# Four row sums moved from TensorE to accumulating DMAs, with the preparation reordered, in a four-layer graph kernel

## The chip, the cores and the metric

The kernel runs on one core of a Trainium2 chip. The metric is device time of one launch, in microseconds; lower is better. The core has five instruction streams that run side by side and meet only at semaphores: TensorE (PE in the profile, with its weight loads as PEld), VectorE (DVE), ScalarE (ACT), GpSimd (POOL) and SyncE (SP). Each stream runs its instructions in the order in which they were written; an instruction that waits holds up everything behind it on its own engine. DMAs are issued by one of these streams and then run on their own.

## The reference

The input is `x`, 32 samples of 512 nodes with 256 features in float32, and one adjacency matrix `adj` (512 x 512, integers). Four layers follow each other; each adds its result to `x` after a layer norm with a ReLU:

```python
h = jnp.maximum(_layernorm(x, axis=-1), 0.0)
x = x + _L3_gnn_ref(h, adj, adj[None], L3_gnn_W, ...)      # layers 0, 1, 2 likewise
```

Layer 0 is masked attention with four heads. Layer 1 is an MLP with two graph attentions. Layer 2 is a graph attention with four heads of 64 features, layer 3 one with eight heads of 32 features and a prior made of `adj`. For each head of layers 2 and 3 the score of a pair of nodes is a sum of two numbers, one of the row and one of the column, under a leaky ReLU:

```python
e = jax.nn.leaky_relu(e_src[..., :, None] + e_dst[..., None, :], ALPHA)
attn = jax.nn.softmax(e, axis=-1)
h = jnp.einsum('bhij,bhjf->bhif', attn, x_proj)
```

## The kernel before

First comes a preparation: it loads the weights, turns `adj` into four masks (`mask1`, `mask0T`, `mask1T`, `mask3T`), multiplies attention vectors into the weights, and computes a flag `go` that says whether the fast path may be taken. Then all engines branch, and `pipelined` runs. (`general`, the other branch, does not run on these inputs.)

In `pipelined` the four layers of each sample are recorded as steps by a planner, `Plan`. The planner puts the steps of all samples into one order by a list schedule of its own: it has a cost for each step (`cost`), release times for samples and layers (`STARTS`, `PACE`, `LAYERS`), due times (`PERIOD`, and the shifts in `URGENT`) and a stock of buffers (`BLOCKS` tiles of 128 x 512 float32, four `x` tiles, eight banks of PSUM). Steps of up to four samples stand interleaved on every engine. `_Recorder.__getattr__` (line 261) records each step and so is the line that the profile shows for all of them; the tiles tell them apart.

Layers 2 and 3 go through `separable`. After the layer norm, `node_major` computes values and scores of 128 nodes at a time; ScalarE copies the scores to the tile `e`. Four transposes bring the row scores to one row a head (`pt<-ident,e`), ScalarE copies them to `rT`, a DMA writes them to DRAM (`rd`), and one DMA a head broadcasts a row to 128 partitions (`R<-rd`). Heads are worked off in groups `g` of four. For each of the four blocks `j` of 128 keys and each head `s`, ScalarE makes `p = exp(R + e)`, VectorE takes the maximum with the other branch of the leaky ReLU and applies the mask (`p<-p,e,mask3T`), and TensorE multiplies with the values: four matmuls of 32 columns each, one a head, run beside each other in the array as one unit ("columns").

The denominators of the softmax are sums over the keys. In group 0, VectorE adds the four `p` of a head into `total`, and TensorE sums `total` over partitions in one unit with a matrix of ones. In group 1, which only layer 3 has, nothing is added beforehand: TensorE runs a unit of four sum matmuls for every `j`, accumulating in the PSUM bank `sm`:

```python
if not added:
    for s in range(4):
        q.tensor.matmul(sm[s * F3 : (s + 1) * F3, :], ones[:, :F3], p[s], **st)
```

`normalise` then copies `sm`, sends it through DRAM for a reciprocal and a broadcast, and multiplies (`oT<-raw,rc`).

In layer 1, `first_gat` needs two numbers a node. TensorE leaves four partial rows each in `part`; four matmuls with the selection matrix `pick` sum them into `f1p`, and VectorE copies the eight columns to `sd`.

GpSimd has only two kinds of steps in the pipeline: the power that ends each layer norm's statistics (`rs<-ve,mhalf`, four a sample) and the addition of a bias to `x` in layer 0 (`x<-x,boa`). VectorE's next step of that norm, `ms`, waits for `rs`, then ScalarE's `h`, then TensorE's transposes `pt<-ident,h`.

A first load of `x` can be issued by SyncE only when the preparation's buffers are free, since the `x` tiles lie in the pool `big`, which is opened where the pool `prep` was.

Of the kernel before, what the change touches and what calls it, by code (L numbers as in the profile page):

```python
# [11 lines left out]
F32 = mybir.dt.float32  # L12
# [18 lines left out]
G = 2  # L31
# [10 lines left out]
PERIOD = 51.0  # L42
STARTS, PACE = (0.0, 8.0, 36.0, 32.0), 110.0
LAYERS = (0.0, 51.0, 151.0, 201.0)

URGENT = {
    "stats:0": 76, "h:0": 358, "mm:0": 3, "sc:0": 60, "p0:0": -99, "av:0": 39, "stats:1": -269, "pt:1": 119,
    "nd:1": -201, "total:1": 12, "av:1": -22, "e:1": -39, "o2:1": 73, "s:1": -189, "pt:2": 15, "e4:2": -44,
    "total:2": 10, "stats:3": -38, "mv:3": -56, "mm:3": -12, "p3:3": -178, "total:3": -169, "sm:3": 86,
    "s1:3": -16,  # L50
}
BLOCKS, KEEP = 60, 2
# [244 lines left out]
def cost(engine, op, args, kw, out):  # L297
# [22 lines left out]
    if engine == "POOL":  # L320
        return (1.0 if n < 16 else 0.683), 0.1
# [7 lines left out]
def gnn_stack_kernel(ctx: ExitStack, tc: tile.TileContext, a: dict, out: bass.AP):  # L329
# [29 lines left out]
    def load_col(name, eng):  # L359

        src = a[name]
        t = const.tile([P, src.shape[0] // P], F32, name=name)
        eng.dma_start(t, T(src, "(k p) -> p k", p=P))
        return t

# [19 lines left out]
    bq8 = const.tile([P, KD], F32, name="bq8")  # L385

# [6 lines left out]
    pick = const.tile([P, 2], F32, name="pick")  # L393
# [9 lines left out]

    prep_stack = ExitStack()
    prep = prep_stack.enter_context(tc.tile_pool(name="prep", bufs=2))
    pp = prep_stack.enter_context(tc.tile_pool(name="prep_psum", bufs=1, space=PSUM))
    with prep_stack, tc.manual_schedule():

        adj = prep.tile([P, NT, N], I32, name="adj", bufs=1)
        nc.gpsimd.dma_start(adj, T(a["adj"], "(t p) j -> p t j", p=P))  # L410
# [3 lines left out]
        nc.sync.dma_start(a2, bass.AP(tensor=src.tensor, offset=src.offset, ap=[[0, P], [1, 2 * F2]]))  # L414
        s3 = load_bcast(prep, "L3_a_src", nc.sync, D)
        d3 = load_bcast(prep, "L3_a_dst", nc.sync, D)
        wq = load_rows("wqT", nc.scalar, D)
        rows = []
        for name in ("bq", "bk"):
            t = prep.tile([1, D], F32, name=f"{name}r")  # L420
            nc.sync.dma_start(t, a[name][None, :])
            rows.append(t)
        for k in range(KD):
            nc.scalar.dma_start(
                T(w3[:, k, H3 : H3 + D], "p (h f) -> p h f", h=H3), T(a["L3_W"][:, k * P : (k + 1) * P, :], "h p f -> p h f")
            )
        wk = load_rows("wkT", nc.scalar, D)
        bt = load_bcast(prep, "beta", nc.sync, 1)
        bq = load_col("bq", nc.sync)
        bk = load_col("bk", nc.sync)  # L430
        afc = load_bcast(prep, "a_fc", nc.sync, 2 * HID)
        wo = load_rows("woT", nc.scalar, D)
        wv = load_rows("wvT", nc.scalar, D)
        wfc = load_rows("W_fc", nc.scalar, HID)
        bo = load_bcast(const, "bo", nc.sync, D)
        bv = load_bcast(const, "bv", nc.sync, D)
        bvc = prep.tile([P, KD], F32, name="bvc")
        nc.sync.dma_start(bvc, T(a["bv"], "(k p) -> p k", p=P))
        ahd = load_bcast(prep, "a_hand", nc.sync, 2 * D)
        b1 = load_col("mlp1_b", nc.sync)  # L440
        b2 = load_col("mlp2_b", nc.sync)
        wh = load_rows("W_hand", nc.scalar, D + 2)
        m1 = load_rows("mlp1_w", nc.scalar, HID)
        m2 = load_rows("mlp2_w", nc.scalar, D)
        w3o = load_rows("L3_WoT", nc.scalar, D)
# [10 lines left out]
        for c in range(2):  # L456
            nc.vector.tensor_reduce(pick[:, c : c + 1], ident[:, c:P:32], axis=AX.X, op=ALU.add)


        top = prep.tile([P, NT], F32, name="top")  # L460
        adjf = prep.tile([P, NT, N], F32, name="adjf", bufs=1)
        for t in range(NT):
            nc.vector.tensor_copy(adjf[:, t, :], adj[:, t, :])
        adjT = []
        for j in range(NT):
            pt = pp.tile([P, N], F32, name="adjT", bufs=NT)
            for t in range(NT):
                nc.tensor.transpose(pt[:, t * P : (t + 1) * P], adjf[:, t, j * P : (j + 1) * P], ident)
            adjT.append(pt)
        for t in range(NT):  # L470
            nc.vector.tensor_reduce(top[:, t : t + 1], adjf[:, t, :], axis=AX.X, op=ALU.max)
            nc.vector.tensor_scalar(mask1[:, t, :], adjf[:, t, :], 0.0, -BIG, op0=ALU.is_le, op1=ALU.mult)


        ab = prep.tile([P, 1], F32, name="ab")
        nc.vector.tensor_scalar(ab, bt, -1.0, None, op0=ALU.mult)
        nc.vector.tensor_tensor(ab, ab, bt, op=ALU.max)
        nc.scalar.activation(ab, ab, AF.Exp, scale=-1.0)
        m3 = [prep.tile([P, N], F32, name="m3", bufs=NT) for _ in range(NT)]
        for j in range(NT):  # L480
            nc.scalar.activation(m3[j], adjT[j], AF.Relu)
        nc.scalar.activation(ab, ab, AF.Ln, bias=one)

        ok = prep.tile([P, NT], F32, name="ok")
        nc.vector.tensor_scalar(ok, top, 0.0, None, op0=ALU.is_gt)
        nc.vector.tensor_scalar(top, top, 0.0, None, op0=ALU.max)
        nc.scalar.activation(top, top, AF.Ln, bias=eps)
        for j in range(NT):
            nc.scalar.activation(m3[j], m3[j], AF.Ln, bias=eps)
        nc.vector.scalar_tensor_tensor(beta, bt, 0.0, ab, op0=ALU.max, op1=ALU.add)  # L490

        for j in range(NT):
            nc.scalar.activation(m3[j], m3[j], AF.Exp, scale=beta)
# [9 lines left out]
        for w, h, f, vs, vd in (  # L503
            (w2, H2, F2, a2[:, 0:1, :].to_broadcast([P, H2, F2]), a2[:, 1:2, :].to_broadcast([P, H2, F2])),
            (w3, H3, F3, T(s3, "p (h f) -> p h f", h=H3), T(d3, "p (h f) -> p h f", h=H3)),
        ):
            project(lambda k: w[:, k, h : h + D], KD, h, f, vs, lambda k: w[:, k, :h])
            project(lambda k: w[:, k, h : h + D], KD, h, f, vd, lambda k: w[:, k, 3 * h + D :])
            nc.vector.tensor_scalar(w[:, :, h + D : 2 * h + D], w[:, :, :h], ALPHA - 1.0, None, op0=ALU.mult)
            nc.vector.tensor_scalar(w[:, :, 2 * h + D : 3 * h + D], w[:, :, 3 * h + D :], ALPHA, None, op0=ALU.mult)  # L510


# [3 lines left out]
        for w, row in zip((wq, wk), rows):  # L516
            gp = pp.tile([64, N], F32, name="gp", bufs=2)
            for h in range(4):
                c = slice(h * 64, (h + 1) * 64)
                for k in range(KD):  # L520
                    nc.tensor.matmul(gp[:, c], w[:, k, c], w[:, k, c], start=(k == 0), stop=False)
                nc.tensor.matmul(gp[:, c], row[:, c], row[:, c], start=False, stop=True)
# [4 lines left out]
        for n in range(2):  # L527
# [5 lines left out]
        gab = prep.tile([64, D], F32, name="gab")  # L533
        nc.vector.tensor_copy(gab, gp[:, :D])
        nc.vector.tensor_tensor(gab, gab, gp[:, D:], op=ALU.mult)
        nc.vector.tensor_reduce(
            tests[:64, 2 * H + 1 : 2 * H + 5], T(gab, "p (h f) -> p h f", h=4), axis=AX.X, op=ALU.add
        )
# [6 lines left out]
        nc.vector.tensor_tensor(tests[:, : 2 * H], sq[:, 0, :], sq[:, 1, :], op=ALU.add)  # L545
        bad = prep.tile([P, NT], F32, name="bad")
# [18 lines left out]
        for j in range(NT):  # L565
            nc.vector.tensor_scalar(mask0T[:, j, :], adjT[j], 0.0, None, op0=ALU.not_equal)
            nc.vector.tensor_scalar(mask1T[:, j, :], adjT[j], 0.0, None, op0=ALU.is_gt)
        nc.vector.tensor_scalar(bq8, bq, 0.125, None, op0=ALU.mult)
# [5 lines left out]
        nc.vector.tensor_tensor(boa, bo, tp[:, :D], op=ALU.add)  # L574
        for j in range(NT):
# [26 lines left out]
    def pipelined(stack):  # L602
# [158 lines left out]
        def first_gat(o1):  # L761
# [10 lines left out]
            f1p = bank("f1p")  # L772
            for t in range(NT):
                q.tensor.matmul(f1p[:, 2 * t : 2 * t + 2], part[:, col(t)], pick, start=True, stop=True)
            q.vector.tensor_copy(T(sd, "p t c -> p (t c)"), f1p[:, : 2 * NT])
# [113 lines left out]
        def separable(xt, w, nh, mask, bars):  # L889
# [3 lines left out]
            e = small(f"e{nh}", NT, 3 * nh)  # L893
            v = blocks("vs", 2)
            for t in range(NT):
                ps = node_major(w, t, hT, nh, D + 2 * nh)
                q.scalar.copy(half(v, t), ps[:, :D])
                q.scalar.copy(e[:, t, : 2 * nh], ps[:, D : D + 2 * nh])
            q.scalar.activation(e[:, :, 2 * nh :], e[:, :, nh : 2 * nh], AF.Exp, scale=1.0 / ALPHA)
            pt = bank("pt")  # L900
            for t in range(NT):
                q.tensor.transpose(pt[:nh, col(t)], e[:, t, :nh], ident)
            rT = block("rT")
            q.scalar.copy(rT[:nh, :], pt[:nh, :])
            rd = q.tile(dram, [H3, N], "rd", 6)
            q.sync.dma_start(rd[:nh, :], rT[:nh, :])
            per = P // f
            for g in range(nh // 4):
# [4 lines left out]
                added = g == 0  # L913
                if added:
                    total = blocks("total", 4)
                else:
                    sm = bank("sm")
                for j in range(NT):
                    p = blocks("p3", 4)
                    for s in range(4):  # L920
                        h = 4 * g + s
                        q.scalar.activation(p[s], R[s], AF.Exp, bias=e[:, j, nh + h : nh + h + 1])
                        q.vector.scalar_tensor_tensor(
                            p[s], p[s], e[:, j, 2 * nh + h : 2 * nh + h + 1], mask[:, j, :], op0=ALU.max, op1=ALU.mult
# [477 lines left out]
```

## Time and profile before

| what | before |
|---|---|
| time, median of 3 runs | 4181.78 us (4181.32 to 4182.27) |
| time of the profiled execution | 4184.13 us |
| its span, from first to last instruction | 4182.3 us |
| TensorE busy | 4059.5 us, 97% |
| VectorE busy | 3312.1 us, 79% |
| ScalarE busy | 3004.7 us, 72% |
| GpSimd busy | 254.8 us, 6% |
| mean DMA rate | 43 GB/s |
| sum matmuls of group 1 (`sm<-p,ones`) | 1024 instructions, 142.1 us busy |
| sum matmuls of `total` (`sm<-total,ones`) | 768 instructions, 104.0 us busy |
| `R<-rd` | 384 DMAs of 256 KB |

Busy time is what an engine spent on instructions; the engines overlap, so the rows do not add up to the span. A float32 matmul against 512 columns shows as two instructions in the profile. An instruction's mean duration is longer than the distance at which the next one starts, because matmuls are pipelined; the distance between starts is what a matmul costs where TensorE is the limit. Idle time of an engine costs nothing unless the chain that ends last runs through it.

### The profile page before, as it was taken

The page shows a single profiled execution, that of the slowest core. Times are in us where ns is not written, and L with a number is a line of the kernel's source. Part 1 is how long each engine was busy: PE and PEld are TensorE (multiplying, and loading weights), DVE is VectorE, ACT ScalarE, POOL GpSimd, SP SyncE. Part 2 cuts the span into 40 slices and gives each one's busy share as a digit, 9 for nine tenths or more (in the row PEclk, how much of TensorE's full clock was granted, in tenths as well). Part 3 has the DMA queues.
Part 4 walks back from the last instruction along what each step waited for, and adds up shares of the span by engine and source line. Part 5 has one row for each costly group of instructions (what it writes and reads, how often), then busy time and mean ns, then how long its engine had stood idle before and what let it go on. Part 6 is the DMA issues. An engine that isn't in the chain of part 4 may idle for free.

```text
span 4182.3 us, 52787 instructions
## 1 busy us (share of the span) xinstructions
PE 4059.5 (97%) x17862; PEld 2068.7 (49%) x17862; DVE 3312.1 (79%) x7018; ACT 3004.7 (72%) x5970; POOL 254.8 (6%) x263
## 2 busy tenths in 40 slices
PE   5999999999999999999999999999999999999986
PEld 3545454554454554455554455554455554455442
DVE  5388877878877878877879877879877878877876
ACT  3467777766777766777766777776777776787774
POOL 1000000000000000000000000000000000000000
PEclk7999999999999999999999999999999999999998
DMA  2001111111110111110111111111111111111111
GB/s 84 11 21 47 47 47 33 49 52 32 47 51 30 49 52 32 47 52 30 49 52 32 47 52 31 47 52 32 47 52 32 46 52 32 47 52 32 41 42 52
DMA packets 149435, 181.07 MB, mean 43 GB/s; under 512 B 45858, under 2 KB 81572, under 8 KB 149156
## 3 DMA queue, kind: packets, MB, share of 16 engines
q1 hardware_dynamic: 143572, 172.37, 13.5%
q10 hardware_dynamic: 5312, 4.20, 0.3%
q8 instruction: 143, 2.34, 0.2%
q14 instruction: 136, 1.11, 0.1%
q0 software_dynamic: 272, 1.05, 0.1%
HBM read 158.41 MB, written 19.14 MB: 42 GB/s over the span
## 4 chain that ended last, share of the span: by engine, by line
PE 78%; DVE 13%; DMA 4%; ACT 2%; issue 1%; SPq 0%; POOL 0%; DVEq 0%; POOLq 0%
PE mm L261 36%; PE av L261 26%; PE pt L261 6%; PE sc L261 5%; PE sm L261 4%; DVE p L261 3%; DVE total L261 3%; DVE ue L261 2%; DMA rc<-s 2%; DVE o L261 2%; PE f1p L261 1%; DVE oT L261 1%; ACT p L261 1%; DVE x L261 1%; DMA s<-few 1%; DMA R<-rd 1%
## 5 line engine op out<-in xcount | busy, mean ns | idle before, releaser
L261 ACT ACTIVATE p<-R,e 128x512 f32<-128x512 f32 x1536 | 1010.2, 721 | 167.7 <-DMA R<-rd 167.5
L261 DVE SCALAR_TENSOR_TENSOR p<-p,e,mask3T 128x512 f32<-128x512 f32 x1024 | 718.2, 745 | 368.1 <-ACT p L261 367.9
L261 PE MATMUL av<-p,v 128*64 128x512 f32 (+1 forms) x2048 | 689.8, 597 | 1.4 <-DVE p L261 1.4
L261 DVE TENSOR_TENSOR total<-total,p 128x512 f32<-128x512 f32 x832 | 547.2, 680 | 0.0
L261 PE MATMUL av<-p,vs 128*32 128x512 f32 (+1 forms) x3072 | 524.8, 598 | 19.2 <-DVE p L261 19.1
L261 PE MATMUL mm<-W_fc,o 128*128 128x512 f32 x1024 | 467.0, 593 | 0.0
L261 PEld LDWEIGHTS av<-p,v 128*64 128x64 f32 (+1 forms) x2048 | 257.5, 163 | 363.4 <-issue 297.1
L261 POOL TENSOR_TENSOR rs<-ve,mhalf 128x4 f32<-128x4 f32 x128 | 151.0, 1180 | 3764.2 <-DVE ve L261 3593.1
L261 DVE SCALAR_TENSOR_TENSOR p<-p,e,mask1T 128x512 f32<-128x512 f32 x512 | 367.6, 742 | 5.8 <-ACT p L261 5.4
L261 ACT ACTIVATE h<-x,ms,rs 128x256 f32<-128x256 f32 x512 | 269.7, 593 | 128.7 <-DVE ms L261 128.7
L261 DVE TENSOR_TENSOR p<-p,mask0T 128x512 f32<-128x512 f32 x512 | 324.1, 681 | 38.3 <-ACT p L261 38.3
L261 PEld LDWEIGHTS av<-p,vs 128*32 128x32 f32 (+1 forms) x3072 | 135.8, 119 | 346.0 <-issue 239.0
L261 PEld LDWEIGHTS mm<-W_fc,o 128*128 128x128 f32 x1024 | 188.9, 190 | 210.0 <-issue 183.4
L261 DVE TENSOR_TENSOR total<-p,p 128x512 f32<-128x512 f32 x416 | 278.9, 678 | 1.0
L261 ACT ACTIVATE p<-sc 128x512 f32<-128x512 f32 x512 | 262.9, 687 | 7.7 <-PE sc L261 7.7
L261 PE MATMUL mm<-w,hT 128*128 128x272 f32 (+1 forms) x1024 | 262.3, 398 | 1.8 <-ACT hT L261 1.8
L261 PE MATMUL av<-pT,v 128*128 128x512 f32 x512 | 239.9, 593 | 0.5 <-ACT pT L261 0.4
L261 PE MATMUL mm<-o,mlp_w 128*128 128x512 f32 x512 | 228.8, 598 | 0.0
L261 PE MATMUL sc<-qT,kT 64*128 64x512 f32 x1024 | 228.3, 595 | 0.0
L261 PE MATMUL mm<-hT,mlp_w 128*128 128x512 f32 x512 | 225.7, 592 | 0.0
L261 PEld LDWEIGHTS mm<-w,hT 128*128 128x128 f32 x1024 | 188.1, 193 | 54.8 <-ACT hT L261 10.3
L261 ACT COPY sums<-sm 128x512 f32<-128x512 f32 x96 | 55.8, 581 | 195.8 <-PE sm L261 195.7
(187 smaller groups left out, 6076.5 us busy)
## 6 DMA issues: line engine op xcount, KB each, us to landing
R<-rd SPq DMA_DIRECT2D x384, 256.0 KB
x<-in_x_dram SPq DMA_DIRECT2D x32, 512.0 KB
rc<-s SPq DMA_DIRECT2D x128, 128.0 KB
rc<-s SPq DMA_DIRECT2D x256, 64.0 KB
out_dram<-x SPq DMA_DIRECT2D x32, 512.0 KB
s<-sums SPq DMA_DIRECT2D x96, 8.0 KB
few<-s SPq DMA_DIRECT2D x96, 8.0 KB
s<-few SPq DMA_DIRECT2D x96, 8.0 KB
```

Of the source, the lines that this page charges most:

```text
L261: getattr(getattr(self.nc, attribute), op)(*args, **kw)
```

## The change

- In group 1 of layer 3, VectorE's four `p` of block 0 become accumulators (`first`). For blocks 1 to 3, GpSimd issues a DMA that adds `p[s]` to `first[s]` in SBUF: 12 DMAs of 256 KB a sample, 384 in all. TensorE sums the accumulators in one unit at the end, as it does with `total` in group 0. An accumulating DMA waits for the matmul that reads `first[s]` as values' weights, for its own `p[s]`, and for the DMA before it on the same `first[s]`.
- In `separable`, the row scores go to a tile of their own (`es`), so that one transpose does for all four node blocks, with a smaller `rT`; the copies from PSUM become two small ones.
- In `first_gat`, four transposes of `part` and a VectorE reduction take the place of the four matmuls with `pick` and the copy.
- In the preparation, `adj` is loaded by SyncE in four pieces, most weights by SyncE and the two `L3_W` pieces by GpSimd; five bias vectors come as one row and are turned by 12 small matmuls; the transposed `adj` is copied to SBUF by ScalarE, and the masks are made from that copy; the projection of `w2` moves ahead of the masks, and `mask1` behind `go`.
- The `x` tiles get a pool of their own (`first`), opened before `prep`.
- The planner's numbers change (`PERIOD`, `STARTS`, `PACE`, `LAYERS`, `URGENT`, 59 blocks for 60), and with them the order of all steps.

```diff
-PERIOD = 51.0
-STARTS, PACE = (0.0, 8.0, 36.0, 32.0), 110.0
-LAYERS = (0.0, 51.0, 151.0, 201.0)
+PERIOD = 54.0
+STARTS, PACE = (0.0, 6.0, 22.0, 46.0), 81.0
+LAYERS = (0.0, 31.0, 185.0, 164.0)
...
-BLOCKS, KEEP = 60, 2
+BLOCKS, KEEP = 59, 2
...
     if engine == "POOL":
+        if op == "dma_start":
+            return 1.2, 3.0
...
+    first = ctx.enter_context(tc.tile_pool(name="first", bufs=1))
...
-        nc.gpsimd.dma_start(adj, T(a["adj"], "(t p) j -> p t j", p=P))
+        av = T(a["adj"], "(t p) j -> p t j", p=P)
+        for t in range(NT):
+            nc.sync.dma_start(adj[:, t, :], av[:, t, :])
...
+        projections(w2, H2, F2, a2[:, 0:1, :].to_broadcast([P, H2, F2]), a2[:, 1:2, :].to_broadcast([P, H2, F2]))
...
+            at = prep.tile([P, N], F32, name="at", bufs=NT)
+            nc.scalar.copy(at, pt)
+            adjT.append(at)
...
+        projections(w3, H3, F3, T(s3, "p (h f) -> p h f", h=H3), T(d3, "p (h f) -> p h f", h=H3))
...
+        for c in range(12):
+            nc.tensor.matmul(cp[:, c : c + 1], row[:, c * P : (c + 1) * P], ones[:1, 0:1], start=True, stop=True)
+        nc.vector.tensor_copy(biases, cp[:, :12])
...
-            f1p = bank("f1p")
-            for t in range(NT):
-                q.tensor.matmul(f1p[:, 2 * t : 2 * t + 2], part[:, col(t)], pick, start=True, stop=True)
-            q.vector.tensor_copy(T(sd, "p t c -> p (t c)"), f1p[:, : 2 * NT])
+            pt = bank("pt")
+            for t in range(NT):
+                q.tensor.transpose(pt[:, col(t)], part[:, col(t)], ident)
+            q.vector.tensor_reduce(sd, T(pt, "p (t k c) -> p t c k", k=KH, c=32)[:, :, :2, :], axis=AX.X, op=ALU.add)
...
-                q.scalar.copy(e[:, t, : 2 * nh], ps[:, D : D + 2 * nh])
+                q.scalar.copy(es[:, t * nh : (t + 1) * nh], ps[:, D : D + nh])
+                q.scalar.copy(e[:, t, :nh], ps[:, D + nh : D + 2 * nh])
...
-            for t in range(NT):
-                q.tensor.transpose(pt[:nh, col(t)], e[:, t, :nh], ident)
-            rT = block("rT")
-            q.scalar.copy(rT[:nh, :], pt[:nh, :])
+            q.tensor.transpose(pt[: NT * nh, :P], es, ident)
+            rT = q.tile(big, [P, P], "rT", 4, tag="turned")
+            q.scalar.copy(rT[: NT * nh, :], pt[: NT * nh, :P])
...
-                        if added and j:
+                        if j and total:
                             q.vector.tensor_tensor(total[s], first[s] if j == 1 else total[s], p[s], op=ALU.add)
-                    if added and not j:
+                        elif j:
+                            q.gpsimd.dma_start(out=first[s], in_=p[s], accum_op=ALU.add)
+                    if not j:
                         first = p
...
-                        if not added:
-                            for s in range(4):
-                                q.tensor.matmul(sm[s * F3 : (s + 1) * F3, :], ones[:, :F3], p[s], **st)
-                if added:
-                    sm = bank("sm")
-                    with q.unit("columns", 0.86):
-                        for s in range(4):
-                            q.tensor.matmul(sm[s * F3 : (s + 1) * F3, :], ones[:, :F3], total[s], start=True, stop=True)
+                sm = bank("sm")
+                with q.unit("columns", 0.86):
+                    for s, b in enumerate(total or first):
+                        q.tensor.matmul(sm[s * F3 : (s + 1) * F3, :], ones[:, :F3], b, start=True, stop=True)
...
-            xt = q.tile(big, [P, NT, D], "x", 4)
+            xt = q.tile(first, [P, NT, D], "x", 4)
```

## The prediction

> **What bounds the kernel now.** I read the page first, then stretches of the steady state, then the chain of waits inside one sample's period, then the groups by form, and last the start in order of time.
>
> The page: span, TensorE's share, its granted clock by slices, and the chain that ended last.
>
> ```profile
> span 4182.3 us, 52787 instructions
> PEclk7999999999999999999999999999999999999998
> PE 78%; DVE 13%; DMA 4%; ACT 2%; issue 1%; SPq 0%; POOL 0%; DVEq 0%; POOLq 0%
> ```
>
> TensorE carries the chain, and its clock is full but for the first and last slices. The stretches (PE, PEld, DVE, ACT, POOL busy, then clock, DMA share and rate):
>
> ```profile
> 400.00:640.00 240.00, 239.31 (x1072) 121.91 (x1071) 195.87 (x418) 180.86 (x363) 15.48 (x16) 1.00 0.14 43
> 3700.00:3890.00 190.00, 188.66 (x878) 94.37 (x877) 160.86 (x326) 141.39 (x279) 9.20 (x9) 1.00 0.13 40
> 4100.00:4183.00 83.00, 53.69 (x216) 22.26 (x208) 46.13 (x91) 31.77 (x62) 1.34 (x1) 0.84 0.17 53
> ```
>
> From 70 to 3890 us TensorE is never free; VectorE has about a fifth of its time left. So work taken from TensorE is time, until VectorE's order or a wait steps in. The period of a sample, from the timeline of TensorE: the sums that close first_gat's softmax start at 2009.39 and again at 2134.51, so 125.1 us a sample.
>
> ```profile
> 2009.39 0.95 PE L261 MATMUL sm<-ones,total 128*128 128x1 f32 x8
> 2134.51 0.95 PE L261 MATMUL sm<-ones,total 128*128 128x1 f32 x8
> ```
>
> The chain between them shows what the parts to be removed cost, start to start (x8 is four matmuls of two passes):
>
> ```profile
> 2091.66 1.00 PE av L261 x8
> 2092.66 0.86 PE sm L261 x8
> 2093.51 0.86 PE av L261 x8
> 2094.37 0.86 PE sm L261 x8
> ...
> 2111.91 0.79 PE f1p L261 x8
> ...
> 2117.95 0.44 PE pt L261 x4
> ```
>
> One unit of four sums is 0.86 us of the path, the `pick` matmuls 0.79, four transposes 0.44. GpSimd's rows by form, the only price for a DMA that it issues:
>
> ```profile
> L261 POOL TENSOR_TENSOR rs<-ve,mhalf 128x4 f32<-128x4 f32 x128 | 151.0, 1180 | 3764.2 <-DVE ve L261 3593.1 <-DMA x<-in_x_dram 61.0 <-ACT y L261 57.1
> L410 POOL DMA_DIRECT2D adj<-in_adj_dram x1 | 0.9, 918 | 0.4 <-issue 0.4
> ```
>
> And the start:
>
> ```profile
> 42.98 0.67 DVE L566 TENSOR_SCALAR mask0T<-adjT 128x512 bf16<-128x512 f32 x1
> ...
> 57.31 2.02 SPq L261 DMA_DIRECT2D x<-in_x_dram  x4
> 61.53 1.41 DVE L261 BATCH_NORM_STATS2 stats<-x 128x6 f32<-128x256 f32 x4 [4.29 <-DMA x<-in_x_dram]
> ...
> 65.57 2.16 PE L261 MATMUL pt<-ident,h 128*128 128x128 f32 x8 [13.71 <-ACT h L261]
> ```
>
> The flag is done at 42.98, but `x` is asked for only when VectorE ends the preparation at 57.2.
>
> **The change, part by part.** Counts are from the order of the two programs' instructions.
>
> TensorE. (a) Sums of group 1: 512 matmuls become 128, that is 96 units of 0.86 us gone: -82.6. (b) Score transposes: 8 a sample become 2; 6 x 0.109 x 32 = -20.9. (c) `pick`: 0.79 becomes 0.44: -0.35 x 32 = -11.2. (d) Changes between full, row and column mode go from 304 to 309, 0.094 us each (the next pass starts 0.429 us after a 512-column one, at a change of mode 0.523): +0.5. Sum -114.2. All of it lies on the path, since TensorE has no free time there. Counted the same way, a sample's TensorE work falls from 122.7 to 119.1 us; the missing 2.4 of the 125.1 are waits.
>
> (e) Waits in the steady state. The new order works in pairs: between the closing sums of successive samples TensorE's work alternates 83.8 and 154.4 us, and VectorE's work between its own same marks 61.0 and 141.2 (before: 122.7 and 101.1 each time). VectorE's free time in the long stretch is 13 us plus the waits, against 24 in 125.1 before. If waits go with length over free time, 2.4 becomes 2.4 x 154.4/125.1 x 24/15.6 = 4.6 in the long and 1.6 in the short stretch, 6.2 a pair against 4.8: +1.4 for each of some 15 pairs, +20. Bounds: all waits gone, -74 (2.4 x 31); waits doubled, +74. I take +20.
>
> (f) The accumulating DMAs. Issue: between 0.92 us (the `adj` row, 1 MB) and, from above, no row; the nearest GpSimd work under load, `rs`, takes 1.18 against 1.04 at the start, so I take 1.0, 12 us a sample on an engine that is 6% busy. Landing: `R<-rd`, the same 256 KB, lets ScalarE start 3.6 us after its first issue at 4124.27; `adj`, four times the bytes and on GpSimd's queue, landed 10.2 us after its issue. I take 5, nearer to the row of the same size, with twice the reading. Cover: in TensorE's order 33.5 to 35 us of work stand between the last values' matmul of group 1 and the sums that need `first`, and 3.2 more back to the matmuls of block 0 that free `first`. Twelve issues and one landing are 12 + 5 = 17 us, or 11 + 10 = 21 by the far row; each is hidden under 36.7. Without that cover each us would cost 32. Only the last two samples have less: 4.6 and 2.0 us, but there group 0 follows with 17.9 us of VectorE work (16 of 0.67, 12 of 0.60) for the last one. Cost 0, at worst +15 at the end.
>
> What is queued behind a waiting DMA on GpSimd is `rs`, and behind that VectorE's `ms` and all after it. The tightest place comes once a pair: six issues and two `rs` stand before a norm whose transposes come 16.2 us of TensorE work after block 0's matmuls: 6 x 1.0 + 2 x 1.18 + 0.7 = 9.1. Hidden; with 10.2 for the landing it is 10.2 + 3 + 1.9 = 15.1, still hidden. VectorE leaves 2.4 us of work between `ve` and `ms`, twice what `rs` takes. SyncE's queue carries as many DMAs as before (1184), and the mean rate goes from 43 GB/s to about 70 with 100 MB more; the broadcasts land later by a little, in ScalarE's free quarter. ScalarE: 8 more small copies of 0.07 and two cheaper ones (0.57 to about 0.2) a sample, no cost. VectorE: a reduction for a copy, under 0.2 us.
>
> A rule that speaks against the change: the Trainium skill, "SBUF — State Buffer", section "A bandwidth-pool intuition that's wrong (but worth ruling out)", has a GpSimd-issued DMA take about 620 ns alone and about 3100 beside a VectorE copy that locks GpSimd's port. With 3.1 us for each issue the formula of the second rival would give 4327. The same page, "Who interferes with whom", lists copies and `tensor_scalar` as the lockers and keeps `tensor_tensor` from stalling the DMAs; then only the four `p<-r,ew` a sample (0.54 us each here) count, and the sum stays. No run here shows which.
>
> (g) The start. Durations from the rows of before in the new order: projections of `w2` (3.4) and `beta` run while `adj` lands (11.5 before); then casts 1.4, `top` 2.8, projections of `w3` 3.4, grams after TensorE's 5.1 and 2.0, the flag near 27. Masks from SBUF 8 x 0.33 (`mask` from `adjf`) for 8 x 0.60 from PSUM, biases and `boa` behind TensorE's 2.0, `mask1` 1.3, `mask3T` 2.4, `prf` 4.9 and 1.4: the end near 42.5 for 57.2, -14.7. `x` is issued after the flag and lands under the masks, so the 4.3 us wait goes; less 1 for the branch: -18. Bounds: 0 if the loads queued on SyncE arrive late (those of before had left ScalarE's queue by 24.75), -23. I take -18.
>
> (h) The end: group 1's sums no longer close the last chain (4155.9 to 4160.6): -3 to +15; I take 0.
>
> Sum: -114.2 + 20 - 18 = -112. The profiled execution took 4184.1 (span 4182.3); the median of the three is 4181.8. I set the change against the median: 4069 us.
>
> **The rivals.** First, VectorE takes its place in the chain: the long stretches leave it 13 us, and if the waits double the sum is 4069 + 54 = 4123. For it: `p<-p,e` waits already turn up in the chain (DVE 13%). Against it: in the middle stretch TensorE stood idle for 0.7 of 240 us.
>
> Second, on the other side: GpSimd's issues are slow beside VectorE, and sums and `rs` come late. With c us an issue, a sample loses 12c + 5 - 36.7 at the sums and a pair 6c + 3.1 - 16.2 at the norm. 32 and 15 times these eat the 112 at c = 2.8; from there it is slower. At 3.0, a little over three times the row, it is 138 + 74 more, 4281. Against it: the 0.92 row; for it: that row is from the start, where VectorE stood still.
>
> Third, the TensorE waits shrink instead, as fewer sums stand between heads: 4069 - 20 - 74 = 3975.
>
> A fourth, that the loads undo the start's gain, gives 4087 and lies inside the first case.
>
> **How the numbers follow.** 0.2% (8 us) is what a measurement of this kernel can tell from no change. The forecast case, 4020 to 4105, has 0.74; the first rival, 4105 to 4173, 0.13; the second, above 4190, 0.07; the third, below 4020, 0.05; within 0.2%, 0.01. So faster 0.92, same 0.01, slower 0.07. The range 4020 to 4140 holds the forecast case and half of the first rival, 0.80.
>
> **What would show it.** Right: `sm<-p` down to 256 instructions, TensorE still near 99% in the middle, two samples in about 244 us, the first `pt<-ident,h` near 47 us, DMA issues on GpSimd near 1 us and no wait of TensorE for them. Wrong: TensorE or VectorE waiting for GpSimd's DMAs or `rs`; VectorE's `p` ahead of `av` in the chain; DMA issues over 2 us. The prediction fails most easily by the waits of (e), which I scaled and did not see.

## The result, and the profile after

The changed kernel takes 4214.8 us (median of 4 runs, 4209.1 to 4223.6) against 4181.6 us for the kernel before: a ratio of 1.0082, with a 95% interval of 1.0064 to 1.0099. It is 0.8% slower. The forecast was 4069 us, with 4020 to 4140 as its range, so the miss is 146 us. The profiled execution took 4214.9 us (span 4213.0), next to the median.

The page of the changed kernel: span, TensorE's granted clock in 40 slices, the chain that ended last by engine.

```profile
span 4213.0 us, 52125 instructions
...
PEclk8999999999999999999999999999999999999998
...
PE 73%; DVE 7%; DMA 7%; ACT 6%; issue 5%; POOL 1%; SPq 0%; DVEq 0%; ACTq 0%; POOLq 0%
```

TensorE has fewer instructions (16,798 matmuls for 17,862) and a smaller share of the chain. Transfers went from 4 to 7% of it, ScalarE from 2 to 6%, and time in which nothing recorded was waited for from 1 to 5%. The stretches say more (the same columns as before: PE, PEld, DVE, ACT, POOL busy, then clock, DMA share and rate):

```profile
400.00:640.00 240.00, 234.03 (x1007) 120.59 (x1007) 202.27 (x439) 180.84 (x381) 43.77 (x42) 0.99 0.30 70
3700.00:3890.00 190.00, 182.40 (x786) 97.25 (x785) 146.30 (x309) 149.68 (x320) 39.16 (x38) 0.98 0.35 80
4130.00:4213.00 83.00, 46.84 (x149) 19.15 (x149) 42.53 (x84) 29.62 (x61) 11.55 (x13) 0.82 0.38 88
```

In 240 us of the steady state TensorE is now idle for 6.0 us (0.7 before), and its granted clock is no longer full. The sums that close first_gat's softmax, in the timeline of TensorE:

```profile
2153.86 1.00 PE L261 MATMUL sm<-ones,total 128*128 128x1 f32 x8
...
2239.02 0.95 PE L261 MATMUL sm<-ones,total 128*128 128x1 f32 x8
...
2408.80 1.02 PE L261 MATMUL sm<-ones,total 128*128 128x1 f32 x8
```

Two samples take 254.9 us (2408.80 - 2153.86), in steps of 85.2 and 169.8. The work in TensorE's order between these marks is 83.8 and 154.4 us, as the prediction counted it. The short stretch is as forecast. The long one loses 15.4 us, where the prediction allowed 4.6. In it TensorE is idle for 7.4 us, and the granted clock falls short by 5.1 us, in small part within the stops. That is where the time went: some 8 us a sample over the counted work in place of 2.4.

What TensorE waits for, from the view of waits by engine (total us, times, longest):

```profile
PE mm L261 <- DVE oT L261: 65.8, 14, 11.4
PE pt L261 <- DVE rs L261: 47.6, 15, 4.2
```

In the same view of the kernel before the first wait is smaller, and the second has no row:

```profile
PE mm L261 <- DVE oT L261: 29.2, 31, 7.4
```

Two stalls, each about once a pair of samples. `woT` holds the output weights of layer 0's attention, and its matmuls read `oT`; first_gat's `rs` is VectorE's reciprocal of the closing sums (GpSimd's `rs` in the layer norms is another tile). Summed over TensorE's timeline from 200 to 3900 us, the idle gaps over 0.15 us are 117 us in all (20 before): 59 ahead of the `woT` matmuls, 44 ahead of the transposes of first_gat's `rs`. And the clock follows most of them down. The two places, in stretches of a few us:

```profile
2230.00:2240.90 10.90, 10.90 (x44) 6.65 (x42) 8.52 (x18) 5.50 (x21) 3.74 (x4) 1.00 1.08 198
2240.90:2243.60 2.70, 0.04 (x1) 0.00 (x0) 1.60 (x3) 2.41 (x4) 0.00 (x0) 1.00 0.50 190
2243.60:2246.00 2.40, 2.34 (x9) 2.01 (x10) 2.20 (x4) 2.40 (x5) 0.00 (x0) 0.58 0.00 0
...
2319.00:2323.30 4.30, 0.08 (x1) 0.02 (x1) 0.83 (x2) 4.30 (x8) 0.00 (x0) 0.91 0.56 128
2323.30:2327.00 3.70, 3.69 (x9) 2.98 (x10) 3.70 (x6) 2.86 (x5) 0.00 (x0) 0.50 0.00 0
2327.00:2330.00 3.00, 3.00 (x10) 2.45 (x9) 0.52 (x2) 0.00 (x0) 0.00 (x0) 0.61 0.00 0
```

TensorE stops for 2.7 us and for 4.3 us, and when work resumes the granted clock is 0.50 to 0.61 for some us. Integrated over 200 to 3900 us, the clock's shortfall is 61 us in the changed kernel, 55 of them outside the gaps themselves, and 0 in the kernel before. 97 us of new idle time and 55 us of shortfall are 152 us, more than the 114 us of counted work that the change takes off TensorE and the 13.5 us of the start (measured below) together. The balance, 24 us longer, is near the 33 measured.

The first row also shows what precedes the `rs` stall: for 11 us the 16 DMA engines are completely busy (share 1.08, as the view adds up the times of packets; 198 GB/s, where the mean over the span is 67). Here are SyncE's transfers and GpSimd's accumulating DMAs around it:

```profile
2232.18 0.63 SPq L261 DMA_DIRECT2D rd<-rT  x1
2236.41 2.64 SPq L261 DMA_DIRECT2D R<-rd  x4
...
2308.82 0.62 SPq L261 DMA_DIRECT2D rd<-rT  x1
2309.54 0.39 SPq L261 DMA_DIRECT2D s<-few  x1
2310.84 3.92 SPq L261 DMA_DIRECT2D R<-rd  x8
2314.86 2.92 SPq L261 DMA_DIRECT2D rc<-s  x4
```

```profile
2220.15 3.59 POOL L261 DMA_DIRECT2D p<-p  x4 [4.61 <-PE av L261]
...
2234.52 1.26 POOL L261 DMA_DIRECT2D p<-p  x1 [0.53 <-DMA p<-p]
```

The train of twelve accumulating DMAs is issued from 2220.15 to 2235.8, and in the middle of it the other sample's layer 2 writes its scores (`rd`, 8 KB) and reads them back (`R`, four broadcasts of 256 KB). `rd` takes 4.2 us until `R` can be issued. The chain of waits goes on from there:

```profile
2236.83 5.06 DMA R<-rd
...
2241.91 0.73 ACT p L261
...
2242.67 0.75 DVE p L261
2243.42 0.10 DVE rs L261
...
2243.66 0.79 PE pt L261 x4
```

`rs` does not need `R`: it stands behind `p` on VectorE because the plan put it there. At the other place, near 2310, no accumulating DMA is in flight (GpSimd's next one is at 2340.7), and none is at any of the 14 `woT` stalls. The four `rc<-s` that release `oT` simply stand behind eight `R<-rd`, 2 MB, on SyncE's queue, and the first of them lands late. The chain of waits there, and below it one row of the chain of the kernel before:

```profile
2315.42 6.93 DMA rc<-s
...
2322.47 0.70 DVE oT L261
...
2323.31 6.66 PE mm L261 x16
```

```profile
2034.20 2.30 DMA rc<-s
```

On SyncE's queue an `rc<-s` comes directly behind `R<-rd` 14 times in the changed kernel, as often as the stall, and never in the kernel before.

### The profile page after: what moved, and what is told of

Its sections match the earlier page's. It is cut to its first block, busy times and chain, and to the rows that moved or that the text cites. A ratio compares the mean times of both kernels' runs of the same rounds, so it can differ in the third digit from the quotient of the medians.

```text
span 4213.0 us, 52125 instructions
## 1 busy us (share of the span) xinstructions
PE 4006.4 (95%) x16798; PEld 2053.8 (49%) x16798; DVE 3306.8 (78%) x7017; ACT 2999.6 (71%) x6230; POOL 668.3 (16%) x648
## 3 DMA queue, kind: packets, MB, share of 16 engines
q0 software_dynamic: 55392, 100.95, 14.3%
q1 hardware_dynamic: 145690, 176.50, 13.3%
## 4 chain that ended last, share of the span: by engine, by line
PE 73%; DVE 7%; DMA 7%; ACT 6%; issue 5%; POOL 1%; SPq 0%; DVEq 0%; ACTq 0%; POOLq 0%
PE mm L261 34%; PE av L261 25%; PE pt L261 6%; PE sc L261 4%; DMA R<-rd 3%; DVE p L261 3%; PE sm L261 3%; DVE total L261 2%; ACT p L261 2%; DMA rc<-s 2%; ACT h L261 1%; POOL rs L261 1%; ACT s L261 1%; ACT e L261 1%; PE f1p L261 1%
## 5 line engine op out<-in xcount | busy, mean ns | idle before, releaser
L261 ACT ACTIVATE p<-R,e 128x512 f32<-128x512 f32 x1536 | 995.2, 727 | 98.1 <-DMA R<-rd 93.5
L261 PE MATMUL av<-p,v 128*128 128x512 f32 (+1 forms) x2048 | 709.0, 604 | 1.3 <-DVE p L261 1.2
L261 POOL TENSOR_TENSOR rs<-ve,mhalf 128x4 f32<-128x4 f32 x128 | 214.2, 1675 | 2767.9 <-DVE ve L261 2578.3
L261 PE MATMUL av<-p,vs 128*32 128x512 f32 (+1 forms) x3072 | 498.9, 597 | 14.1 <-DVE p L261 14.0
L261 POOL DMA_DIRECT2D p<-p x384 | 354.6, 1210 | 670.5 <-PE av L261 547.3
L261 PEld LDWEIGHTS av<-p,v 128*128 128x128 f32 (+1 forms) x2048 | 266.8, 167 | 371.6 <-issue 321.2
L261 DVE SCALAR_TENSOR_TENSOR p<-p,e,mask1T 128x512 f32<-128x512 f32 x512 | 349.8, 744 | 67.1 <-ACT p L261 67.0
L261 DVE TENSOR_TENSOR oT<-raw,rc 128x512 f32<-128x512 f32 x128 | 87.6, 692 | 227.3 <-DMA rc<-s 222.4
L261 ACT COPY v<-mm 128x512 f32<-128x512 f32 (+1 forms) x320 | 156.0, 499 | 145.2 <-PE mm L261 138.8
L261 PE MATMUL mm<-o,mlp_w 128*128 128x512 f32 x512 | 243.1, 595 | 0.0
```

What stands on the lines that cost most here:

```text
L261: getattr(getattr(self.nc, attribute), op)(*args, **kw)
```

## The experiments

Three theories at the start. O: the new order itself sets the waits. C: the accumulating DMAs crowd the DMA engines. M: both, each at its own stall. Each round of runs had runs of the kernel before on the same chip (4182.5 to 4184.8 us, 4181.6 beside the change), so a difference between kernels of different rounds is uncertain by up to 3 us from that alone.

**Four runs on the two stalls.** The first kernel keeps the planned order and issues no accumulating DMA:

```diff
             for step in self.order():
                 for attribute, op, args, kw in step.calls:
+                    if attribute == "gpsimd" and op == "dma_start":
+                        continue
                     getattr(getattr(self.nc, attribute), op)(*args, **kw)
```

> The changed kernel with its order on every engine kept, only that GpSimd issues none of the 384 accumulating DMAs; group 1's sums then hold one key block of four. Theory C (the accumulating DMAs crowd the DMA engines, and all that waits for SyncE's transfers comes late): both stalls of a pair go, the idle 117 us between 200 and 3900 us and the halved clock behind it, 4050 to 4080 us. Theory O (the new order itself sets the waits): nothing moves, 4205 to 4215. Theory M (the stall of the transposes of rs1 needs the accumulating DMAs in flight, the stall of the matmuls of woT comes of the order on SyncE's queue alone): 44 us of idle time and some 36 of halved clock go, 4215 - 80 = 4135 us (4110 to 4155), and the woT stall stays near 4 us once a pair.

The second keeps every DMA, its waits and its place, with 16 of 512 columns:

```diff
+                    if attribute == "gpsimd" and op == "dma_start":
+                        kw = dict(kw, out=kw["out"][:, :16], in_=kw["in_"][:, :16])
```

> The changed kernel with its order kept, each accumulating DMA moving only 16 of the 512 columns (8 KB for 256 KB; the same 128 rows, and the same waits on GpSimd); the other columns of group 1's sums lack three key blocks of four. If bytes do the harm: as without the DMAs, within 10 us of that run. If the issue on GpSimd, its waits or the number of packets do it: near 4215 us.

The third moves only the `rc<-s` steps on SyncE's queue, in the finished order:

```diff
-            for step in self.order():
+            for step in self.rc_first(self.order()):
...
+        for i, s in enumerate(queue):                # SyncE's steps, in order
+            if name(s) != "rc":
+                continue
+            j = i
+            while j and name(queue[j - 1]) == "R" and queue[j - 1] not in s.before:
+                j -= 1
+            if j < i:                                # ahead of the R<-rd right before it
+                queue.insert(j, queue.pop(i))
...
```

> The changed kernel, the same result; on SyncE's queue alone the four broadcasts rc<-s go ahead of the R<-rd that stand right before them. Theory O and theory M: rc lands some 4 us sooner, the woT stall (59 us idle, some 36 us of halved clock behind it) goes, 4215 - 95 = 4120 us (4095 to 4145), and the stall at rs1 stays. Theory C: rc stays late because the DMA engines are busy, less than 30 us gained, above 4185 us.

The fourth has the third's edit and the first's:

> Both edits at once (group 1's sums hold one key block of four). Theory M: the gains add, 4215 - 80 - 95 = 4040 us (4015 to 4065), the time forecast for the change without its grown waits. Theory C: as without the DMAs alone. Theory O: as rc first alone.

Measured: without the DMAs 4136.2 us, with small ones 4135.4, `rc` first 4201.6, `rc` first without the DMAs 4104.8.

Theory M's 4135 for the first was met, and the small DMAs settle what does the harm: with all 384 issues, waits and 128 rows each in place, but 1/32 of the bytes, the whole 79 us is gone. The same stretch of SyncE's timeline without the DMAs, and the load of the DMA engines there:

```profile
2196.41 0.65 SPq L263 DMA_DIRECT2D rd<-rT  x1
2198.32 1.75 SPq L263 DMA_DIRECT2D R<-rd  x4
```

```profile
2194.00:2204.00 10.00, 10.00 (x41) 6.13 (x39) 9.68 (x20) 7.31 (x25) 0.00 (x0) 1.00 0.34 107
```

`rd` lets `R` go after 1.9 us instead of 4.2, the DMA engines are a third busy, TensorE is busy for all of the 10 us, and the stall at `rs` does not occur. Over the whole run `R` goes out more than 3 us after its `rd` 16 times in the changed kernel, and not once when the DMAs are left out or small. The gaps ahead of the `woT` matmuls stay, 60 us, as theory M had it.

The gain of `rc` first was badly over-expected: 13 us, not 95, and with the DMAs left out 31, so that theory M's 4040 for the fourth run was missed as well. By its number `rc` first fits theory C (less than 30 us gained), but not by its waits: `rc` does come sooner. They say why so little came of it:

```profile
PE pt L279 <- DVE rs L279: 50.2, 15, 4.2
PE av L279 <- ACT pT L279: 40.4, 14, 4.7
```

The `woT` stall went, and at the same place another appeared, of nearly the same size: `av<-pT` waits for ScalarE's copies `pT`, and these stand behind the first exponential that reads `R`, which now lands later. At that place two late transfers lay on top of each other, and mending one uncovers the other.

**Moving the readers of R.** The planner takes 1.6 us + bytes/190 GB/s for a transfer on SyncE's queue, which is 3.0 us for `R`, and so it puts work that reads `R` early. In `rc_first_r_late` the first exponential of each layer's first group that reads `R`, with all that depends on it, goes behind whatever the plan starts within 3 us of it:

```diff
-            for step in self.rc_first(self.order()):
+            for step in self.rc_first(self.r_late(self.order(), 3.0)):
...
+            while j < len(steps) and steps[j].start < p.start + by:
+                s = steps[j]
+                if any(id(b) in late for b in s.before) or (...):   # or: a later exponential of the layer
+                    late.add(id(s))
+                    late_list.append(s)
+                else:
+                    early.append(s)
+                j += 1
+            steps[i:j] = early + late_list
```

> The changed kernel with rc first on SyncE's queue and, besides, the first exponential of each group of heads that reads R (and all that depends on it) put behind whatever the plan starts within 3 us of it on any engine, so that the copies pT, the reciprocal rs and their like no longer stand behind a transfer that is late. Same result. Theory M2 (the grown waits are the plan's: it sets work that reads R ahead of other work on ScalarE and VectorE for a landing that it takes to be 2 to 6 us sooner than it is; the accumulating DMAs lengthen that landing): the stalls at rs and at pT, 86 us idle in rc_first and 60 to 70 us of halved clock behind them, go; 4202 - 145 = 4055 us (4035 to 4090). Rival (the DMA engines are too full, the wait only moves to the exponentials' readers): above 4150 us.

> The changed kernel with only the readers of R put later (by 3 us of the plan), SyncE's queue as in the change. Same result. The stall of the rs transposes goes (44 us idle, some 36 of halved clock), the woT stall behind rc stays near 4 us a pair: 4215 - 80 = 4135 us (4115 to 4160). If the two edits only help together: above 4185 us.

> As the kernel with both order edits, but 5 us in place of 3. Same result. If waits for R still make up what is lost against the forecast (4120 against 4069): 4085 to 4110 us. If what is left has other causes (the norm's rs on GpSimd, VectorE's queue): 4115 to 4135 us.

Measured: both edits 4120.2 us, the readers of `R` alone 4190.9, both with 5 us 4148.5.

| accumulating DMAs | order of the change | `rc` first | `R` late | both |
|---|---|---|---|---|
| issued | 4214.8 | 4201.6 | 4190.9 | 4120.2 |
| left out | 4136.2 | 4104.8 | not run | 4071.4 |

Each edit alone gives 13 and 24 us, both together 95. So the order of the queues around late transfers is a cause, and 4120 is between the two theories stated for it (4055 and over 4150): something is left. The kernel with both edits computes the whole result and is faster than both kernels of this study, at 0.9849 of before (0.9833 to 0.9866). The 5 us version is worse than that of 3: what is moved further back is late for others. `r_late` missed its 4135 and met its alternative, that the two edits only help together (above 4185); `both_5us` missed both of its ranges.

**The DMAs in the mended order.**

> The kernel with both order edits (rc first, and what reads R late) at 4120 us, now without the accumulating DMAs (group 1's sums hold one key block of four). If the DMAs cost only by making a badly placed wait longer, little is left to gain: 4100 to 4120 us. If they still delay transfers that TensorE waits for: 4040 to 4080 us.

4071.4 us: the DMAs still cost 49 us with both edits in. TensorE's waits with both edits, the DMAs issued:

```profile
PE pt L306 <- ACT h L306: 38.3, 25, 10.9
PE mm L306 <- DVE oT L306: 22.9, 7, 11.1
```

Of the first, 27 us lie between 200 and 3900 us as gaps of 1.6 to 2.6 us once a pair. Without the DMAs these are 2.6 us in all. And the closing sums without the DMAs:

```profile
1839.96 0.95 PE L308 MATMUL sm<-ones,total 128*128 128x1 f32 x8
...
1924.87 0.95 PE L308 MATMUL sm<-ones,total 128*128 128x1 f32 x8
...
2083.35 0.95 PE L308 MATMUL sm<-ones,total 128*128 128x1 f32 x8
```

243.4 us for two samples, where 244 was forecast for the change.

**Where in the train the harm sits.** In the order of the change, the first four or the last four of a group's twelve DMAs are left out:

```diff
+                        done[name] = done.get(name, 0) + 1
+                        if done[name] == 1:          # no_block1; 3 in no_block3
+                            continue
```

> The changed kernel with its order kept; of a group's twelve accumulating DMAs the last four, those of key block 3, are not issued (group 1's sums lack that block). If only what is in flight when the next sample's rd and R are issued does harm: nearly all of the 79 us comes back, 4135 to 4155 us, and the stall of the rs transposes goes. If all traffic does harm alike: a third of 79, about 4189 us.

> The changed kernel with its order kept; of a group's twelve accumulating DMAs the first four, those of key block 1, are not issued (group 1's sums lack that block). If only what is in flight when rd and R are issued does harm: little comes back, 4200 to 4217 us, and the stall of the rs transposes stays. If all traffic does harm alike: about 4189 us.

4133.6 us without block 3, 4129.5 without block 1: either third of the bytes brings back all of the 79 us. That refutes "all traffic does harm alike" (4189 for both). The expectation for block 1 was wrong, for a reason that the timelines of GpSimd and SyncE show. Without block 3:

```profile
2189.23 0.86 POOL L267 DMA_DIRECT2D p<-p  x1 [0.56 <-DMA p<-p]
```

```profile
2192.86 0.63 SPq L267 DMA_DIRECT2D rd<-rT  x1
2194.76 1.75 SPq L267 DMA_DIRECT2D R<-rd  x4
```

Each accumulating DMA into a block waits for the one before into the same block, so leaving out the first four moves the rest forward. Without block 1 the last issue is at 2189.66 and `rd` at 2193.27; without block 3 it is 2189.23 and 2192.86. In both the last DMA is issued some 3.6 us ahead of `rd`, and `R` follows `rd` by 1.9 us; in neither run does `R` go out more than 3 us after `rd`. In the change the last was issued 2.3 us after `rd`. What counts is whether the train is still being issued when `rd` goes out; where between 3.6 us ahead and 2.3 us behind the harm begins was not measured.

**A shorter train with the whole result.** The adds of one key block go to VectorE, in the kernel with both order edits:

```diff
+                        if done[name] == 1:          # both_dve_block1; 3 in both_dve_block3
+                            self.nc.vector.tensor_tensor(kw["out"], kw["out"], kw["in_"], op=ALU.add)
+                            continue
```

> The kernel with both order edits (4120 us), the adds of key block 1 of group 1 done by VectorE (four of about 0.68 us a sample) in place of their accumulating DMAs, at the same place of the order. Same result. If the collision with rd and R makes up the 49 us: the train ends before rd, 4071 us plus what VectorE's 2.7 us a sample cost where it has 20% of its time free, 4075 to 4105 us. If something else does: 4115 to 4150 us.

> The same with key block 3, the last of the train. The train ends as early, but VectorE's four adds stand behind the landing of the DMAs of block 2, in the middle of its queue. If VectorE's order is hurt by it: 4120 to 4170 us; if the adds wait for nothing: as the run with block 1.

4150.2 and 4166.9 us; the collision theory had 4075 to 4105 for the first. Over the run `R` now goes out more than 3 us after `rd` 14 times, as often as in this order without any DMAs (there `rc` stands between the two), and no longer 30 times as with all twelve. The gaps ahead of `pt<-h` fall from 27 us to 4 and 1. So the collision went, and by TensorE's gaps and clock it was the larger part of the 49 us; no run shows that in the time. But the four adds, 87 us of VectorE's time in the whole run (32 x 4 x 0.68), and the eight DMAs that are left cost 79 us against the kernel without DMAs (4150 - 4071). New stalls stand in their place: 14 us ahead of first_gat's `mx`, or 27 us ahead of the sums. VectorE has a fifth of its time free on average and hardly any where the adds went: from 5 us before to 5 us after a group's four adds it is 99% busy with block 1's and 97% with block 3's (medians of 32). This does not beat 4120.

**The parts of the change alone, and new plans.** The kernel before with only the new preparation, whose samples keep the order of before:

> The kernel before with the new preparation and x's own pool alone; the order of the samples' work on TensorE, ScalarE and VectorE is that of before. By step (g) of the prediction: -18 us against before. By the first closing sum of the changed kernel, which started only 8 us sooner against the work ahead of it: -8 us.

4169.0 us, -13.5 (0.9966, 0.9954 to 0.9979), between the 18 and the 8 expected. The first `pt<-ident,h` of this kernel, and of the changed one:

```profile
50.94 2.17 PE L261 MATMUL pt<-ident,h 128*128 128x128 f32 x8 [10.95 <-ACT h L261]
```

```profile
51.23 2.17 PE L261 MATMUL pt<-ident,h 128*128 128x128 f32 x8 [10.94 <-ACT h L261]
```

It starts 14.3 us earlier than before (65.57) in the changed kernel.

Three kernels were planned anew. Two put group 1's sums back on TensorE and keep the rest of the change (with `rT` in a block of 128 x 512), once with the planning numbers of before and once with those of the change. One leaves the change as it is and corrects the prices of transfers:

```diff
         if op == "dma_start":
-            return 1.2, 3.0
+            return 1.2, 4.5
...
-    return 0.4, 1.6 + size / 190e3
+    return 0.4, 2.2 + size / 100e3
```

> The changed kernel without the accumulating DMAs: group 1's sums on TensorE as before, es and rT and the transposes for pick as in the change, the new preparation, and the planning numbers of before (rT in a block). Same result. TensorE's work falls by 32 us (steps b and c); with the start it is 4185 - 32 - 8 to 18 = 4135 to 4145 us if the waits stay those of before. If a new order by itself brings waits, whatever the numbers: above 4165 us.

> The changed kernel with group 1's sums on TensorE as before in place of the accumulating DMAs, planned anew with the numbers of the change (same result; the run with the numbers of before gave 4548). TensorE's work is 83 us more than in the change, and no accumulating DMA is in flight. If the numbers of a plan suit one set of steps only: above 4300 us. If the numbers of the change are good for this one too: 4215 - 79 + 83 = 4219 us or less.

> The changed kernel with two lines of the plan's prices changed and all orders planned anew from them: a transfer on SyncE's queue lasts 2.2 us + bytes at 100 GB/s (1.6 us + bytes at 190 GB/s before; 4.8 us for 256 KB, where the profile of the changed kernel shows 5.1), an accumulating DMA 4.5 us after its issue (3.0 before; profile 5.5 from issue). Same result. Theory M2: the waits shrink, 4040 to 4120 us. If the waits come of crowded DMA engines whatever the plan: 4190 to 4230 us.

4547.6, 4610.4 and 4224.8 us. The first was expected at 4135 to 4145 or, if a new order by itself brings waits, above 4165. The second met one of its two cases: above 4300 if a plan's numbers suit one set of steps only. The third missed the 4040 to 4120 of better prices, and its number lies in the range for crowded DMA engines (4190 to 4230). The first has by count 32 us less work on TensorE than before and is 365 us slower. Over its whole run TensorE is idle for 280 us (118 before), waits for VectorE's `p` the longest, and the clock falls short by 112 us (49 before); the rest of its loss was not taken apart. The third, priced nearer to what the profile shows, has other waits (`pt<-p` 32 us, `av<-p` 25) in place of the old. The planning numbers suit one set of steps and prices, and a new order from other steps is another kernel. These runs don't separate the parts of the change; they show how much the order can cost, which the prediction had put at +-74 us.

## Why the prediction was wrong, point by point

The sum again, with what the runs put in the place of each term:

| step | forecast | measured |
|---|---|---|
| (a) to (d), TensorE's work | -114 | not timed alone, taken as -114; see below |
| (g), the start | -18 | -13.5 |
| (e), waits of the new order | +20 | +82 |
| (f), accumulating DMAs | 0 | +79 |
| sum | -112 | +33 |

The +82 is 4136.2 (order of the change, no DMAs) less 4181.8 - 114.2 - 13.5 = 4054; the +79 is 4214.8 - 4136.2. The +82 is thus a remainder, but TensorE's own timeline agrees: without the DMAs it has 57 us more idle time than before and 24 to 27 us of missing clock between 200 and 3900 us. With both order edits the two become 17 and 49.

**(a) to (d).** The count held: `sm<-p` is down to 256 matmuls. The kernel with both edits and no DMAs runs two samples in 243.4 us where the prediction had 244, and ends at 4071 where it had 4069. TensorE is busy for 3961.3 us there and for 4068.1 in `prep_alone`, 107 us less for the 114 counted. So the work did go. That 4071 and 4069 agree to 2 us is partly luck: the start gave 4.5 us less than its term and the waits 3 us less than theirs. That TensorE is the bound was right too, but what it lost in work it gained in waits.

**(e) failed, as the step that was said to be the weakest.** The prediction scaled the waits by the length of a stretch over VectorE's free time in it. The waits that came are of another kind: a step that needs a late transfer stands ahead of one that doesn't, on an in-order queue, and TensorE waits for the second. This has nothing to do with how busy VectorE is. The working even had what was needed: the planner counts 3.0 us for `R` where the trace had 3.6, and the two orders could be laid side by side, which shows `rc<-s` behind eight `R<-rd` on SyncE, and `pT` and `rs` behind the readers of `R`. The bounds (+-74) were no bounds either: they assumed that waits could at most double, and +82 lies outside. The base was misread as well. The 2.4 us a sample that the count of work left over were called waits, but TensorE was idle for 0.6 us of the 125.1 of the sample shown, and for 20 us in all from 200 to 3900; most of the 2.4 lies in TensorE's busy time, and so there were no 74 us of waits to lose.

**(f) was right in its parts and wrong in one sentence.** The DMA's price was right:

```profile
L261 POOL DMA_DIRECT2D p<-p x384 | 354.6, 1210 | 670.5 <-PE av L261 547.3 <-DMA p<-p 75.2 <-DVE ve L261 21.6
```

1.21 us on GpSimd in the mean (median 0.9) for the 1.0 taken, a landing of 5.5 us for the 5 taken, and TensorE waits for these DMAs for 1.8 us in all, at the very end. The figure weighed in the prediction (3.1 us an issue beside VectorE) was not met: the longest issue took 2.3 us. What failed is "the broadcasts land later by a little, in ScalarE's free quarter". That was read from the mean rate, 43 against 70 GB/s. The DMA engines are full while a train runs (a share of 1.08 over 10.9 us), and there `R` goes out 2.3 us later behind `rd` and lands later. What that brought was +79 where the term was 0. ScalarE's free quarter doesn't help: the waiting exponential holds up what stands behind it.

**(g)** was mis-sized. The preparation ended at 47.0 us, not 42.5, and `x` landed in time as forecast; 14.3 us at the first transposes became 13.5 in the time.

**(h)** held: the last wait for `oT` is 11.4 us where before it was 7.4 and 1.5, and no more than that.

**The rivals.** The second had the right side for the wrong reason: GpSimd's issues are not slow. The first, VectorE in the chain, is not what the change shows; the runs with four adds on VectorE come nearer to it. What was missing is a rival in which SyncE's transfers come late, which the order of its queue would have suggested.

The page "TensorE: Matmul & The Clock Gate" of the Trainium skill (section "Part 1: The HAM clock gate (the "warmup" mystery)") has the clock fall to half after an idle window of about 3.4 us and come back after as long a busy one. The rows of the two places agree for the stop of 4.3 us, which was followed by a clock of 0.50; the stop of 2.7 us, shorter than that window, was followed by one of 0.58 as well. The granted clock stayed at half for 3.4 us at the shorter stop and for 6.8 at the longer one.

## What to carry to other kernels

When a change moves an order that a planner writes, compare the two orders queue by queue around every transfer: which step on an in-order engine waits for a landing, by how much the planner's price for it is too short, and what stands behind that step that doesn't need it. A transfer that nobody waits for can still cost what others' transfers lose while it is under way; look at the DMA engines in the stretch in which it runs, not at the mean rate. And where TensorE is the bound, as here, a stop of 3 us or more cost about 2 us more than its length, by the shortfall of the clock.

## What was not expected of the hardware

- Stops of TensorE and the clock. Over all 18 traces, between 200 and 3900 us, the granted clock fell during or within 3.5 us after 12 of 337 stops of 0.5 to 1.5 us, 79 of 147 stops of 1.5 to 3 us, and 156 of 160 of 3 us and more; after the end of these longest its shortfall was 2.1 us each. All 12 of the short ones are in the three kernels that were planned anew, next to other gaps within some us.
- The packets of an accumulating DMA hold the DMA engines about twice as long per byte as those of the other transfers. By the table of queues of the changed kernel (packets, MB, share of 16 engines' span), it is 14.3% for 100.95 MB against 13.3% for 176.50 MB, a factor of 1.9; packets of 2 KB alone take 193 ns against 100 in the mean, the same factor:

```profile
q0 software_dynamic: 55392, 100.95, 14.3%
q1 hardware_dynamic: 145690, 176.50, 13.3%
```

- Twelve of them, 3 MB of sums, therefore take all 16 engines for about 19 us (0.143 x 4213 / 32 = 18.8), a little longer than GpSimd takes to issue them (2220.15 to 2235.8), and the sixteen are full from 2221 to 2236.5 (share 1.05). That points to the engines, and not to GpSimd's issues, as what sets the train's length.
